# Two masked-attention layers in overlapped turns: layer 1's statistics and norms moved into the next turn, the second reciprocal behind the last addition

## The chip, the core and the metric

The kernel runs on one core of one Trainium2 chip. The metric is device time in microseconds (us). Five engines matter: PE (TensorE, the matrix products; its weight loads are listed as PEld), DVE (VectorE), ACT (ScalarE), POOL (GpSimd) and SP (SyncE), which issues every DMA of this kernel. Each engine works through its own instructions in the order in which the program lists them, and waits at an instruction until what that one needs is there. So an instruction that waits holds up everything behind it on its engine.

## What is computed

The input `x` is 128 graphs of 128 nodes with 512 features, `adj` is a 0/1 mask of 128x128 for each graph. Two layers follow one another; cut to what matters they are

```
# layer 0: 4 heads of 64; mask = adj
q, k, v = x @ Wq, x @ Wk, x @ Wv
x = layernorm(x + softmax(where(mask, q k^T / 8, -max)) v @ Wo + bo)
# layer 1: 8 heads of 64; mask = adj | identity
h = (x - mean) * rsqrt(var + eps) * gamma + beta
q, k, v = split(h @ w_qkv^T)
x = layernorm(x + softmax(where(mask, q k^T / 8, -1e9)) v @ w_out^T + b_out)
```

All arithmetic is in 32-bit floats.

## The kernel before

**Groups and turns.** Two graphs make a group, so there are 64 groups. The loop runs over turns `s`. One turn works on several groups at different stages, which are independent of one another: layer 0's q, k, v of group s (`product_0`), layer 0's scores and softmax of group s-1 (called part 0), layer 0's attention output and norm of group s-2, layer 1's q, k, v of group s-3 (`qk`, `v`), layer 1's scores and softmax of group s-4 (parts 1 and 2, one for each graph), and layer 1's output of group s-5. `opening` fills the pipeline, `step(s)` runs for s = 2 to 63, `closing(s)` for s = 64 to 66, and `last` ends it. From turn 6 on `step` has all its stages; those 58 turns are most of the time.

**The order is written out by hand.** The scheduler is off (`tc.manual_schedule()`), so the order of the calls in `step` is the order of the instructions on each engine. A buffer that is given again (a pool's tag with its number of buffers) makes its new writer wait for the old readers, DMAs included.

**Products in seven parts.** Every large product is cut into quarters and done with seven half-sized products instead of eight (numbers 1 to 7). `INTO` says in which PSUM bank each is summed: 1, 6, 7 and 4 are summed one after another in bank "a", 5 and 3 in "f", 2 in a bank of its own. After each product somebody takes the partial sum out of the bank: so 4 may start only when the sum of 7 has been read. For the output products (`out_product`, PE on line 498) the reader is DVE, which adds the bank to the rows `R[g]` (line 502). For `product_0` (PE on line 460) ACT copies 1, 6, 5 and 4 (lines 469, 471) and DVE adds 2, 7 and 3 (line 474). For layer 1's `qk` and `v` (line 338) ACT and DVE share it likewise (lines 347, 374, 362). In the profile the output product 4 is `oa<-wso,aT`, and product 4 of `product_0` is `a<-xT,ws` and `a<-ws,xT`.

**Softmax.** `masked` (DVE, line 565) copies the scores out of PSUM under the mask, `maxima` (DVE, line 571) takes row maxima, `exps` (ACT, line 580) eight exponentials for each part in two halves with their row sums, `normalised` a reciprocal of the sums (DVE, line 588) and a multiplication (POOL, line 589). `blocks` transposes blocks of 32 on DVE (line 604) and `put`s them to memory (SP, line 214, `scrp`); `probs_arrive` fetches them in transposed order in four DMAs (SP, line 220, `pT`). Layer 1's k and q go the same way (`scrk`, `kt`, `scrq`, `rawq`), and `q_in_order` (ACT, line 412) puts q in order for the next turn's scores of part 1 (`sc_a`, line 536). The rows of x and of layer 0's result are turned in the same manner by `turn` (DVE, line 229) and fetched by `arrive` (`raw`). The tiles that `turn` and `blocks` write share one tag with two buffers, taken in turn: `blocks(s, 1)` writes the buffer that `blocks(s, 0)` put to memory.

**Statistics and norms.** `stats(l, g, b)` is one `bn_stats` and one `bn_aggr` on DVE (lines 682, 683) for graph b of the group; after b = 1 `roots` computes the scale and the shift in four short POOL instructions (lines 690 to 705). `norms` is put on a list, `later`, and issued by the next `flush()`: two ACT instructions (line 716) and, for layer 1, the DMA of the finished rows to the output (SP, line 719). `step` has two flushes: in the old order the first writes layer 1's norms of the turn before, the second layer 0's of this turn. `load_rows(s - 1)` (SP, line 80) reads x again into one of five row buffers, the one whose rows that output DMA has just written out, so it waits until that DMA has landed. `with_self` (DVE, line 544) adds the diagonal to a mask. `finish` (ACT, line 268) prepares layer 1's input, `addend` (POOL, line 671) adds the bias to the rows.

Of the kernel before, what the change touches and what calls it, by code (L numbers as in the profile page):

```python
# [27 lines left out]
def kernel(ctx: ExitStack, tc: tile.TileContext, x, adj, wq, wk, wv, wo, bo,  # L28
# [4 lines left out]
    NG = B // G  # L33
# [23 lines left out]
    def flush(what=later):  # L57
        while what:
            what.pop(0)()
# [17 lines left out]
    def load_rows(g):  # L77
        if 0 <= g < NG and g not in R:
            R[g] = five.tile([P, G, E], F32, tag="r", name=f"r_{g}")
            nc.sync.dma_start(R[g], x[g * G:(g + 1) * G].rearrange("b n e -> n b e"))  # L80
# [178 lines left out]
    def finish(g, half):  # L259

        if not 0 <= g < NG:
            return
        raw = RAW[1]
        if half == 0:
            XT[1, g] = one.tile([P, KC, T], F32, tag="xT1", name=f"xT1_{g}")
        xT = XT[1, g]
        for c in range(half * KH, (half + 1) * KH):
            nc.scalar.activation(xT[:, c, :].rearrange("p (b a j) -> p b a j", b=G, a=4),
                                 raw[:, :, :, c, :].rearrange("p a b j -> p b a j"),
                                 AF.Identity, bias=gb[:, KC + c:KC + c + 1], scale=gb[:, c:c + 1])  # L270
        if half == 1:
            sums(1, g)
# [268 lines left out]
    def with_self(g):  # L541

        if 0 <= g < NG:
            nc.vector.tensor_tensor(M[g], M[g], eye[:, None, :].to_broadcast([P, G, N]), op=ALU.max)

    def cleared(s, *parts):

        for part in parts:
            if group_of(s, part) is not None:
                sm = SM[part] = one.tile([P, 2, K1, N], F32, tag=f"sm{part}", name=f"sm{part}_{s}")  # L550
                nc.gpsimd.memset(sm, NEG1 if part else NEG0)  # L551
# [22 lines left out]
    def exps(s, part, *halves):  # L574
        if group_of(s, part) is None:
            return
        sm, nmax, total = SM[part], NMAX[part], TOTAL[part]
        for i in halves:
            for k in range(K1):
                nc.scalar.activation(sm[:, i, k, :], sm[:, i, k, :], AF.Exp, bias=nmax[:, i, k:k + 1],  # L580
                                     accum_out=total[:, i, k:k + 1])

    def normalised(s, *parts):
        for part in parts:
            if group_of(s, part) is None:
                continue
            rec = one.tile([P, 2, K1], F32, tag=f"rec{part}", name=f"rec{part}_{s}")
            nc.vector.reciprocal(rec, TOTAL[part])  # L588
            nc.gpsimd.tensor_tensor(SM[part], SM[part], rec[:, :, :, None].to_broadcast([P, 2, K1, N]),  # L589
                                    op=ALU.mult)  # L590
# [7 lines left out]
    def blocks(s, *parts):  # L598


        for part in parts:
            if group_of(s, part) is not None:
                t = one.tile([P, 4, 2 * K1 * 32], F32, tag="turned", bufs=2, name=f"turnedp{part}_{s}")
                nc.vector.transpose(t.rearrange("p q (h r) -> p q h r", r=32),  # L604
                                    SM.pop(part).rearrange("p i k (q r) -> p q (i k) r", r=32))
                SCR["p", part] = put(t, f"scrp{part}_{s}")
# [50 lines left out]
    def out_sums(l, g):  # L657
        if not 0 <= g < NG:
            return
        K = HEADS[l] // 2  # L660
        so = SO[l, g] = one.tile([P, 4, K // 2, N], F32, tag=("qo0", "xs0")[l], name=f"so{l}_{g}")
        halves_sums(so, AT[l, g].rearrange("p b (h c) n -> p b h c n", h=2))
# [13 lines left out]
    def stats(l, g, b):  # L676
        if not 0 <= g < NG:
            return
        if b == 0:
            MV[l, g] = two.tile([P, G, nc.vector.BN_AGGR_DIM], F32, tag="mv", name=f"mv{l}_{g}")  # L680
        st = three.tile([P, nc.vector.BN_STATS_DIM], F32, tag="st", name="st")
        nc.vector.bn_stats(st, R[g][:, b])
        nc.vector.bn_aggr(MV[l, g][:, b], st)  # L683
        if b == G - 1:
            roots(l, g)
# [125 lines left out]
    def step(s):  # L811

        made = scores(s)
        load_ahead(s + 1)
        if s > 2:
            in_order(s)
            sums(0, s)
        arrive(1, s - 3)
        masked(made, s, 0, 1, 2)
        attend(s)  # L820
        maxima(s, 0, 1)
        out_sums(0, s - 2)
        exps(s, 0, 0)
        product_0(s, 1)
        exps(s, 0, 1)
        out_product(0, s - 2, 1, 2, 5)
        maxima(s, 2)
        product_0(s, 2)
        flush()
        load_rows(s - 1)  # L830
        normalised(s, 0)
        out_product(0, s - 2, 6, 3)
        exps(s, 1, 0)
        stats(0, s - 2, 0)
        product_0(s, 6)
        exps(s, 1, 1)
        normalised(s, 1)
        finish(s - 3, 0)
        out_product(0, s - 2, 7)
        product_0(s, 5)  # L840
        out_product(0, s - 2, 4)
        blocks(s, 0)
        stats(0, s - 2, 1)
        exps(s, 2, 0)
        product_0(s, 7)
        finish(s - 3, 1)
        exps(s, 2, 1)
        product_0(s, 3)
        turn(0, s + 1)
        normalised(s, 2)  # L850
        product_0(s, 4)
        if s in (2, 3):
            prepare(len(setup) - (s == 2))
        blocks(s, 1)
        probs_arrive(s, 0)
        qk(s - 3, 1)
        if s == 2:
            weight_sums(w1qk, wsqk, 1)
            prepare(1)
        flush()  # L860
        qk(s - 3, 2)
        blocks(s, 2)
        arrive(0, s + 1)
        probs_arrive(s, 1)
        qk(s - 3, 6, 5)
        flush(latest)
        addend(1, s - 5)
        out_sums(1, s - 5)
        qk(s - 3, 7, 3, 4)
        k_arrive(s - 3, 0)  # L870
        probs_arrive(s, 2)
        turn(1, s - 2)
        out_product(1, s - 5, 1, 2)
        q_arrive(s - 3)
        v(s - 3, 1, 2)
        k_arrive(s - 3, 1)
        cleared(s + 1, 0, 1, 2)
        out_product(1, s - 5, 6)
        v(s - 3, 6, 5)
        out_product(1, s - 5, 5)  # L880
        v(s - 3, 7, 3)
        out_product(1, s - 5, 7)
        q_in_order(s - 3)
        v(s - 3, 4)
        out_product(1, s - 5, 3, 4)
        addend(0, s - 1)
        stats(1, s - 5, 0)
        stats(1, s - 5, 1)
        with_self(s - 2)
        if s == 2:  # L890
            weight_sums(w1v, wsv, 0, 1)
        if s == 3:
            weight_sums_out(1)

    def closing(s):

        made = scores(s)
        arrive(1, s - 3)
        masked(made, s, 0, 1, 2)
        attend(s)  # L900
        maxima(s, 0, 1)
        finish(s - 3, 0)
        out_sums(0, s - 2)
        exps(s, 0, 0)
        out_product(0, s - 2, 1, 2, 5)
        maxima(s, 2)
        flush()
        load_rows(s - 1)
        finish(s - 3, 1)
        qk(s - 3, 1)  # L910
        exps(s, 0, 1)
        out_product(0, s - 2, 6, 3)
        qk(s - 3, 2)
        normalised(s, 0)
        exps(s, 1, 0)
        out_product(0, s - 2, 7, 4)
        stats(0, s - 2, 0)
        stats(0, s - 2, 1)
        qk(s - 3, 6)
        exps(s, 1, 1)  # L920
        addend(1, s - 5)
        out_sums(1, s - 5)
        qk(s - 3, 5)
        normalised(s, 1)
        exps(s, 2, 0)
        blocks(s, 0)
        flush()
        qk(s - 3, 7)
        exps(s, 2, 1)
        turn(1, s - 2)  # L930
        blocks(s, 1)
        probs_arrive(s, 0)
        qk(s - 3, 3)
        normalised(s, 2)
        flush(latest)
        cleared(s + 1, 0, 1)
        qk(s - 3, 4)
        probs_arrive(s, 1)
        out_product(1, s - 5, 1, 2)
        k_arrive(s - 3, 0)  # L940
        q_arrive(s - 3)
        k_arrive(s - 3, 1)
        blocks(s, 2)
        if s < NG + 2:
            v(s - 3, 1)
        out_product(1, s - 5, 6, 5)
        if s < NG + 2:
            v(s - 3, 2, 6, 5)
        out_product(1, s - 5, 7)
        probs_arrive(s, 2)  # L950
        out_product(1, s - 5, 3, 4)
        q_in_order(s - 3)
        if s < NG + 2:
            v(s - 3, 7, 3, 4)
        stats(1, s - 5, 0)
        stats(1, s - 5, 1)
        cleared(s + 1, 2)
        addend(0, s - 1)
        with_self(s - 2)
# [46 lines left out]
    for s in range(NG, NG + 3):  # L1006
        closing(s)
# [30 lines left out]
```

## Time and profile before

| | us |
|---|---|
| median of 3 runs | 3039.32 (3038.34 to 3039.86) |
| time of the profiled execution | 3041.11 |
| its span, first to last instruction | 3039.3 |
| PE busy | 2838.4 (93%) |
| DVE busy | 1927.0 (63%) |
| POOL busy | 1744.8 (57%) |
| ACT busy | 1543.1 (51%) |
| 16 DMA engines, mean busy share of the one queue | 62.7% |

The profile is of one execution. Its page gives sums over the span; the trace behind it can be asked for the waits of each engine, for the rows of one engine in a stretch of time, and for the busy times, the granted PE clock and the share of the DMA engines in any stretch. In rows of the timeline the columns are start, duration, engine, line, operation, what is written from what, shapes, count, and in brackets the idle time of the engine just before and what ended it. Durations of neighbouring instructions overlap a little, so where a chain is added up here, it goes by the distance from one start to the next.

### The profile page before, as it was taken

The page shows a single profiled execution, that of the slowest core. Times are in us where ns is not written, and L with a number is a line of the kernel's source. Part 1 is how long each engine was busy: PE and PEld are TensorE (multiplying, and loading weights), DVE is VectorE, ACT ScalarE, POOL GpSimd, SP SyncE. Part 2 cuts the span into 40 slices and gives each one's busy share as a digit, 9 for nine tenths or more (in the row PEclk, how much of TensorE's full clock was granted, in tenths as well). Part 3 has the DMA queues.
Part 4 walks back from the last instruction along what each step waited for, and adds up shares of the span by engine and source line. Part 5 has one row for each costly group of instructions (what it writes and reads, how often), then busy time and mean ns, then how long its engine had stood idle before and what let it go on. Part 6 is the DMA issues. An engine that isn't in the chain of part 4 may idle for free.

```text
span 3039.3 us, 54138 instructions
## 1 busy us (share of the span) xinstructions
PE 2838.4 (93%) x18077; PEld 2234.4 (74%) x18077; DVE 1927.0 (63%) x3545; ACT 1543.1 (51%) x4871; POOL 1744.8 (57%) x2311
## 2 busy tenths in 40 slices
PE   8899999999999999999999999999999999999987
PEld 7677777777777777777777777777777777777766
DVE  6566666666666666666666666666666666666644
ACT  3355455454554554554554545545545545445444
POOL 4455555655655655555556556556555555565554
PEclk9999999999999999999999999999999999999998
DMA  5666766756657657667567567676675675675541
GB/s 169 186 178 187 216 183 187 214 177 194 211 178 202 199 178 216 185 185 217 183 184 216 179 191 210 178 205 197 179 216 183 187 218 181 187 213 177 166 141 61
DMA packets 482790, 570.93 MB, mean 188 GB/s; under 512 B 60872, under 2 KB 383440, under 8 KB 482512
## 3 DMA queue, kind: packets, MB, share of 16 engines
q1 hardware_dynamic: 482512, 567.46, 62.7%
q8 instruction: 145, 2.38, 0.3%
q14 instruction: 133, 1.09, 0.1%
HBM read 304.09 MB, written 263.19 MB: 187 GB/s over the span
## 4 chain that ended last, share of the span: by engine, by line
PE 67%; ACT 17%; DVE 7%; issue 3%; SPq 2%; DMA 2%; POOL 2%; ACTq 0%; POOLq 0%; DVEq 0%
PE qka L338 14%; ACT sm L580 12%; PE oa L498 8%; PE qkf L338 7%; PE a L460 6%; PE va L338 6%; PE av L650 6%; PE qkc L338 4%; PE of L498 3%; PE vf L338 3%; ACT r L716 3%; PE f L460 2%; DVE nmax L571 2%; SPq L220 2%; PE sc L536 2%
## 5 line engine op out<-in xcount | busy, mean ns | idle before, releaser
L580 ACT ACTIVATE sm<-sm,nmax 128x128 f32<-128x128 f32 x1536 | 596.4, 393 | 56.2 <-POOL so L302 43.0
L589 POOL TENSOR_TENSOR sm<-sm,rec 128x1024 f32<-128x1024 f32 x192 | 364.0, 1896 | 342.7 <-DVE rec L588 342.7
L671 POOL TENSOR_TENSOR r<-r,bias 128x1024 f32<-128x1024 f32 x128 | 301.2, 2353 | 222.1 <-ACT r L670 222.1
L690 POOL TENSOR_SCALAR ve<-mv 128x2 f32<-128x2 f32 x191 | 41.4, 217 | 562.1 <-DVE mv L683 556.7
L347 ACT COPY ev<-va 128x256 f32<-128x256 f32 x128 | 47.6, 372 | 513.4 <-PE va L338 513.4
L502 DVE TENSOR_TENSOR r<-oa,r 128x256 f32<-128x256 f32 x508 | 206.2, 406 | 152.0 <-PE oa L498 142.0
L580 ACT ACTIVATION_READ_ACCUMULATOR sm<-sm,nmax 128x1 f32 x1536 | 294.4, 192 | 0.0
L412 ACT ACTIVATE qo<-rawq 128x512 f32<-128x512 f32 x124 | 71.3, 621 | 350.3 <-DMA rawq<-scrq 350.3
L502 DVE TENSOR_TENSOR r<-of,r 128x256 f32<-128x256 f32 x254 | 107.3, 422 | 217.7 <-PE of L498 211.1
L498 PE MATMUL oa<-wso,aT 128*128 128x256 f32 x380 | 111.5, 403 | 138.8 <-DVE r L502 138.8
L604 DVE STREAM_TRANSPOSE turnedp<-sm 128x1024 f32<-128x1024 f32 x189 | 229.1, 1212 | 18.6 <-POOL sm L589 15.3
L338 PE MATMUL qkf<-w,xs 128*128 128x512 f32 x496 | 233.2, 592 | 0.5 <-ACT eqk L347 0.5
L338 PE MATMUL qka<-wsqk,xs 128*128 128x512 f32 x496 | 233.1, 592 | 0.0
L571 DVE TENSOR_REDUCE nmax<-sm 128x8 f32<-128x1024 f32 x192 | 226.5, 1206 | 0.2
L302 POOL TENSOR_TENSOR xs<-xT 128x256 f32<-128x256 f32 x256 | 186.7, 729 | 69.1 <-ACT xT L256 37.6
L498 PE MATMUL oa<-wso,so 128*128 128x256 f32 x760 | 210.0, 386 | 12.6 <-DVE r L502 7.9
L498 PE MATMUL of<-wo,so 128*128 128x256 f32 x760 | 209.8, 386 | 0.9 <-POOL so L302 0.7
L716 ACT ACTIVATE r<-r,shift,root 128x512 f32<-128x512 f32 x254 | 192.2, 805 | 0.4 <-POOL shift L705 0.4
L498 PEld LDWEIGHTS oa<-wso,aT 128*128 128x128 f32 x380 | 67.7, 191 | 157.8 <-DVE r L502 151.0
L338 PEld LDWEIGHTS qkf<-w,xs 128*128 128x128 f32 x496 | 94.2, 190 | 119.4 <-issue 117.9
L338 PEld LDWEIGHTS qka<-wsqk,xs 128*128 128x128 f32 x496 | 94.3, 190 | 118.2 <-issue 117.7
L551 POOL MEMSET sm<- 128x1024 f32 x192 | 175.1, 951 | 0.0
(178 smaller groups left out, 7178.7 us busy)
## 6 DMA issues: line engine op xcount, KB each, us to landing
scrp<-turnedp SPq DMA_DIRECT2D x189, 512.0 KB, 3.1
pT<-scrp SPq DMA_DIRECT2D x756, 128.0 KB, 3.6
scr<-turned SPq DMA_DIRECT2D x125, 512.0 KB, 3.6
raw<-scr SPq DMA_DIRECT2D x500, 128.0 KB, 3.6
r<-in_x_dram SPq DMA_DIRECT2D x63, 512.0 KB, 3.6
out_dram<-r SPq DMA_DIRECT2D x63, 512.0 KB, 2.8
scrk<-tk SPq DMA_DIRECT2D x124, 256.0 KB, 3.0
scrq<-tq SPq DMA_DIRECT2D x62, 512.0 KB, 3.8
```

The lines of the kernel that those rows point to most:

```text
L302: nc.gpsimd.tensor_tensor(o, a0, a1, op=op)
L338: nc.tensor.matmul(o, lhsT, rhs, start=first and m == 0, stop=m == len(todo) - 1, skip_group_check=True)
L460: nc.tensor.matmul(acc[:, at * P:(at + 1) * P], lhsT, rhs, start=first and n == 0, stop=n == len(todo) - 1, skip_group_check=True)
L498: nc.tensor.matmul(acc, left[:, c], right[:, c], start=first and c == 0, stop=c == hk - 1, skip_group_check=True)
L502: nc.vector.tensor_add(part, acc, part)
L571: nc.vector.tensor_reduce(NMAX[part], SM[part], AX.X, ALU.max, negate=True)
L580: nc.scalar.activation(sm[:, i, k, :], sm[:, i, k, :], AF.Exp, bias=nmax[:, i, k:k + 1], accum_out=total[:, i, k:k + 1])
L589: nc.gpsimd.tensor_tensor(SM[part], SM[part], rec[:, :, :, None].to_broadcast([P, 2, K1, N]), op=ALU.mult)
L604: nc.vector.transpose(t.rearrange("p q (h r) -> p q h r", r=32), SM.pop(part).rearrange("p i k (q r) -> p q (i k) r", r=32))
L650: nc.tensor.matmul(pm[i * D:(i + 1) * D, at, :].rearrange("p (a r) -> p a r", r=32), v, pT[:, :, i * K1 + at, :], start=True, stop=True)
L671: nc.gpsimd.tensor_tensor(R[g], R[g], (bias0, bias1)[l][:, None, :].to_broadcast([P, G, E]), op=ALU.add)
L716: nc.scalar.activation(R[g][:, b], R[g][:, b], AF.Identity, bias=shift[:, b:b + 1], scale=root[:, b:b + 1])
```

## The change

It reorders `step` and adds two calls to `closing`; no instruction is added, removed or changed in kind.

- Layer 1's `stats` no longer stand at the end of turn s (for group s-5) but in turn s+1 (there group s-6), behind the output products 6 and 3 of layer 0. The first `flush()` with its norms and output DMA, and `load_rows`, move from before `normalised(s, 0)` to behind the output product 4 of layer 0.
- `normalised(s, 1)`, and `finish(s - 3, 0)` with it, move from before the output product 7 to the same place, behind the output product 4.
- Layer 0's first `stats` move from before `product_0(s, 6)` to beside the second, and `blocks(s, 0)` moves behind both and behind `exps(s, 2, 0)` in the text.
- `with_self` moves from the turn's end to before layer 1's output product 6.
- `closing(64)` does the statistics that turn 63 used to do.

```diff
@@ step(s)
         product_0(s, 2)
-        flush()
-        load_rows(s - 1)
         normalised(s, 0)
         out_product(0, s - 2, 6, 3)
         exps(s, 1, 0)
-        stats(0, s - 2, 0)
+        stats(1, s - 6, 0)
+        stats(1, s - 6, 1)
         product_0(s, 6)
         exps(s, 1, 1)
-        normalised(s, 1)
-        finish(s - 3, 0)
         out_product(0, s - 2, 7)
         product_0(s, 5)
         out_product(0, s - 2, 4)
-        blocks(s, 0)
+        flush()
+        load_rows(s - 1)
+        normalised(s, 1)
+        finish(s - 3, 0)
+        stats(0, s - 2, 0)
         stats(0, s - 2, 1)
         exps(s, 2, 0)
+        blocks(s, 0)
         product_0(s, 7)
...
         cleared(s + 1, 0, 1, 2)
+        with_self(s - 2)
         out_product(1, s - 5, 6)
...
         out_product(1, s - 5, 3, 4)
         addend(0, s - 1)
-        stats(1, s - 5, 0)
-        stats(1, s - 5, 1)
-        with_self(s - 2)
@@ closing(s)
         out_sums(0, s - 2)
+        if s == NG:
+            stats(1, s - 6, 0)
+            stats(1, s - 6, 1)
         exps(s, 0, 0)
```

## The prediction

> **What bounds the kernel now.** I read the list of waits of PE first, because the page has PE busy 93% of the span and a matrix engine that full can only be helped where it stands still. Over the 58 full turns (6 to 63, from 193.7 to 2875.6 us by the starts of each turn's first score product, line 531: 2681.9 us, 46.24 a turn) it names one place that counts. Columns: engine, line, who is waited for, us in total, times, longest.
>
> ```profile
> PE oa L498 <- DVE r L502: 133.1, 57, 2.8
> PE a L460 <- DVE qkv L474: 6.2, 26, 0.2
> PE sc_a L536 <- ACT qo L412: 2.2, 6, 0.7
> ```
>
> PE waits some 2.3 us in each turn before an output product, for DVE's addition. Nothing else on PE is near that. The third line matters later: q for part 1's scores comes just in time already.
>
> Next the timeline of PE and DVE around one such wait.
>
> ```profile
> 1546.36 0.61 PE L460 MATMUL f<-w,xs 128*128 128x128 f32 x4
> 1549.20 0.98 PE L498 MATMUL oa<-wso,aT 128*128 128x256 f32 x2 [2.23 <-DVE r L502]
> ```
>
> ```profile
> 1544.97 0.69 DVE L682 BATCH_NORM_STATS2 st<-r 128x6 f32<-128x512 f32 x1
> 1545.70 0.18 DVE L683 BATCH_NORM_AGGREGATE mv<-st 128x2 f32<-128x6 f32 x1
> 1548.65 0.20 DVE L588 RECIPROCAL rec<-total 128x8 f32<-128x8 f32 x1 [2.77 <-ACT sm L580]
> 1548.77 0.37 DVE L502 TENSOR_TENSOR r<-oa,r 128x256 f32<-128x256 f32 x1
> ```
>
> PE has the sum of product 7 ready at 1545.64. Its addition stands on DVE behind part 1's reciprocal, which waits 2.77 us for ACT's exponentials. So product 4 waits for ACT, through DVE's order. ACT works without a break from 1540.20 to then, with layer 1's norms (1.41 us from start to start) in between.
>
> The wait costs twice. The stretches with the granted clock (first column of the kind "1.00" after the busy times) show it:
>
> ```profile
> 1546.07:1549.48 3.41, 1.18 (x10) 0.99 (x9) 0.49 (x2) 3.41 (x15) 0.57 (x2) 1.00 0.42 156
> 1549.48:1552.89 3.41, 3.41 (x16) 3.26 (x16) 2.38 (x5) 3.41 (x15) 1.54 (x2) 0.50 0.48 184
> ```
>
> A stretch of 3.41 us with PE busy for 1.18 of it is followed by one at half clock. Of the 58 turns 31 have such a stretch and take 46.76 us; 27 have none and take 45.63. Cut in such stretches of 3.41 us from 300 to 2850 us, the trace has 0.45 as the least busy share of PE before a full-clock stretch, and 0.43 as the highest before a half-clock one. A gap under 1.9 us can't bring a stretch that low.
>
> On this the Trainium skill differs ("TensorE: Matmul & The Clock Gate", section "HAM oscillation — how this bites in real kernels"): it asks for idle gaps over about 3.4 us before the clock falls, and no gap here reaches that. By it the 31 slow stretches would have another cause and stay, and the forecast below would be worse by 31 x 1.13 = 35 us. The row above decides against it.
>
> **The change, part by part.** T is the start of output product 4 on PE. A turn at full clock is 45.63 us, with PE idle 2.51 before T (1501.04 to 1503.55 in that turn) and 0.24 before `product_0`'s product 4; so 42.87 us are PE's own.
>
> *The wait at T.* Behind product 3's addition DVE now does layer 1's statistics instead of layer 0's first and the reciprocal. Both graphs take 1.61 us (1533.26 to 1534.87, start to start). From 1544.97 that is 1546.58; the addition of 7 starts there, and PE follows such an addition by 0.43 (1548.77 to 1549.20): 1547.01, where PE ends `product_0`'s product 5 at 1546.97. At the turn's start the same statistics (and `with_self`, 0.31) no longer stand before `masked`: score sums are ready at 1533.97 and `masked` started at 1535.18, so DVE gains up to 1.1 us there. I take 0 for the wait at T; the bounds are 0 and 0.1. The exponentials of part 1 lose the norms before them, end about T+0.2, and the reciprocal now reaches DVE at T+1.04, so it no longer waits.
>
> *The next wait: `product_0`'s product 4.* What DVE does between the last addition and the one that this product waits for grows. From T: two products 0.60, their addition starts at T+0.64; reciprocal +0.40; both of layer 0's statistics +0.12; `blocks(s, 0)` +1.61; the addition of `product_0`'s 7 +1.16 (1504.63 to 1505.79); PE +0.59 (1506.58 to 1507.17). Sum T+4.52. PE is there at T+3.28 (3.62 before, less the 0.24 wait and 0.10 by which the first products after an idle stretch were slower, 0.70 against 0.60). New gap 1.24 us, bounds 0.9 and 1.5 by start-to-start steps of 0.35 to 0.46 for an addition. It is under 1.9, so the clock stays.
>
> *ACT and POOL.* Layer 1's shift comes out of POOL 1.92 us after the second aggregate's start, near T+1.4; norms until T+2.85, `finish` 0.98, exponentials 1.55, `finish` 0.99, exponentials 1.55, two copies (0.45, 0.58): T+8.95. `qk` product 6 needs the last copy at T+9.39. Slack 0.4, so hidden; without it every further us would cost PE one. POOL's four sums for `qk` (0.8 apart) start at T+6.4 and the one that product 6 needs is done by T+8. Hidden. `with_self` falls into DVE's 0.37 us of idle before output product 6's addition.
>
> *The DMA queue.* This is what the change may pay with. SP's rows around T:
>
> ```profile
> 1545.23 0.39 SPq L719 DMA_DIRECT2D out_dram<-r  x1
> 1548.91 0.39 SPq L80 DMA_DIRECT2D r<-in_x_dram  x1
> 1551.82 0.34 SPq L214 DMA_DIRECT2D scrp<-turnedp  x1
> 1556.04 0.34 SPq L214 DMA_DIRECT2D scr<-turned  x1
> 1557.24 0.32 SPq L214 DMA_DIRECT2D scrp<-turnedp  x1
> ```
>
> The row load waits for the output DMA to land (median 2.84 us from issue to issue), at a time when SP has nothing else to do. Now the output DMA goes at T+2.9, the load at T+5.75, and part 0's `scrp`, whose tile is ready at T+3.95, stands behind it: T+6.2 instead of T+2.34. It lands 2.6 us later when alone (`scrp` at 1505.89) and 4.2 when packed (`x` at 1531.57): T+8.8 to T+10.4, I take 9.6. Only then may `blocks(s, 1)` write the same buffer on DVE (1.2 us; before, T+5.25): part 1's `scrp` at T+10.9 instead of T+6.46. From there SP has 7.7 us of issues before `scrq` and `scrk` and 0.4 between them: the second `scrk` at T+19.3. Its data are there at T+18.92 (T+18.03 before, plus 0.9 as PE's part from T to there grows). From this `scrk` to q's landing SP and the DMA engines have no hole (the engines are 0.98 busy from 1519 to 1533), and q had 0.1 us to spare (ready 1533.87, PE there at 1533.97). So late here is late on PE: 0.3 us by the middle, 0 by the quick landing, 1.1 by the slow one. Two more DMAs of 512 KB, out and in, now share the engines with this traffic; I add 0.2. I take 0.5.
>
> *Sum.* 42.87 + 0 + 1.24 + 0.5 = 44.61 us a turn; 58 turns 2587.4 against 2681.9: 94.5 less. Turns 4 and 5 have the moved reciprocal too; PE's waits of this kind before turn 6 come to 4.2 us in all, which I leave out. `closing(64)` gains 1.6 us of DVE work that turn 63 loses: between 0 and 1.6, taken as 0. Span 3039.3 - 94.5 = 2944.8, the profiled execution's own time 3041.1 - 94.5 = 2946.6; the runs' median of 3039.32 lies 1.8 below that execution, so **2945 us** for the median.
>
> **The rivals.**
>
> *The queue takes it without delay.* For: SP idles 1.0 us before `scrq` and 0.6 before part 2's `scrp`, and puts alone land in 2.6. Then a turn is 44.11 and the time 2916. Against: the load sits directly before the `scrp`.
>
> *Slower: the row load blocks SP's queue.* One mechanism: the load's wait for the output DMA, now behind T, pushes the `scrp` puts, then the fetches, and with them q past the start of the scores. Price 58 us for each us that q is late. The gain is eaten when q is 46.24 - 44.11 = 2.13 us late. With the slow landing (T+10.4) and 1.5 us more from bursts that share the DMA engines, q is 2.6 late: 46.71 a turn, 3067. For it: engines without a hole from 1519 to 1533. Against: before T they are nearly idle (busy share 0.15 from 1538 to 1544), and SP's own slack takes the first part.
>
> *The new gap hides too.* If PE's order or ACT's copies keep PE back elsewhere, or DVE's chain is 1.2 shorter, only 42.87 + 0.5 remain: 2872 at best. Against: each row of that chain was measured.
>
> *It doesn't do what it says.* The wait at T could belong to something else than the reciprocal. The row with 2.77 us of idle and the release by ACT directly before it excludes that nearly; if ACT's exponentials then held `product_0` through its copies, the turn would stay near 46.2 and the time near 3037.
>
> **How the numbers follow.** Forecast, 2930 to 2985: 0.50. Queue without delay, 2905 to 2930: 0.23. New gap hidden, below 2905: 0.05. q later by 1.2 to 2.0, 2985 to 3033: 0.07. No change: 0.05. Slower by the queue: 0.10. The range from 2900 to 3010 leaves out the hidden gap, half of the late q and the last two, 0.2 in all. A measurement of this kernel can tell about 0.2%, 6 us, from no change. Faster 0.85, same 0.05, slower 0.10.
>
> **What would show it.** In the new trace: DVE's reciprocal of part 1 without idle time before it; no wait of PE at `oa<-wso,aT` and one of 0.9 to 1.5 us at `a<-xT,ws` for DVE's `qkv`; no stretch at half clock in the full turns, so a mean clock near 1.00; `scrp` behind the row load, some 3.9 us later after T than now, and DVE's second `turnedp` waiting for its landing; PE's wait at `sc_a` for ACT's `qo` up from 2.2 us to about 29 in total. I am wrong if that last one is over 120 us, or if ACT's copies release PE in `qk`.

## The result and the profile after

The changed kernel takes 3261.62 us (median of 4 runs, 3257.28 to 3268.38) against 3038.83 us: a ratio of 1.0741, 95% interval 1.0715 to 1.0768. It is slower by 223 us, where the forecast was 2945 us, faster by 94, with a range up to 3010.

The waits of PE in the full turns of the profile after (192.0 to 3094.4 us, 50.04 a turn; columns as before):

```profile
PE sc_a L536 <- ACT qo L412: 219.7, 57, 5.1
PE a L460 <- DVE qkv L474: 64.6, 58, 1.5
```

The wait before the output product 4, 133.1 us before, is gone from the list, as meant. The wait for DVE at `product_0`'s product 4 is 1.11 us a turn. But PE now waits 3.8 us in each turn at `sc_a` for q, where it waited 2.2 us in all. The stretches around one such wait say what else it costs (after the busy times: granted clock, DMA share, GB/s):

```profile
1496.50:1499.90 3.40, 0.00 (x0) 0.00 (x0) 1.33 (x2) 0.00 (x0) 0.00 (x0) 1.00 0.95 222
1499.90:1503.30 3.40, 2.58 (x23) 2.58 (x25) 0.41 (x1) 2.44 (x5) 0.69 (x1) 0.53 0.70 229
1503.30:1506.70 3.40, 3.40 (x34) 3.17 (x34) 3.04 (x5) 0.12 (x1) 2.17 (x4) 0.50 0.29 83
```

PE stands still through a whole stretch, with the DMA engines 0.95 busy, and then runs at half clock for two. The full turns hold 57 such slow spells, 20 of one stretch and 37 of two, 5.5 us a turn at half clock; before it were 31, all of one stretch, and 1.8 us.

Where q's lateness comes from is read from SP's and DVE's rows of one turn (T, the start of output product 4 on PE, is 1516.49):

```profile
1519.25 0.40 SPq L719 DMA_DIRECT2D out_dram<-r  x1
1522.07 0.39 SPq L80 DMA_DIRECT2D r<-in_x_dram  x1
1522.55 0.42 SPq L214 DMA_DIRECT2D scrp<-turnedp  x1
1523.06 0.38 SPq L214 DMA_DIRECT2D scr<-turned  x1
1528.86 0.32 SPq L214 DMA_DIRECT2D scrp<-turnedp  x1
```

```profile
1517.47 0.19 DVE L588 RECIPROCAL rec<-total 128x8 f32<-128x8 f32 x1
1519.15 1.23 DVE L604 STREAM_TRANSPOSE turnedp<-sm 128x1024 f32<-128x1024 f32 x1
1524.27 0.20 DVE L588 RECIPROCAL rec<-total 128x8 f32<-128x8 f32 x1 [1.78 <-ACT sm L580]
1527.59 1.25 DVE L604 STREAM_TRANSPOSE turnedp<-sm 128x1024 f32<-128x1024 f32 x1 [3.12 <-DMA scrp<-turnedp]
```

Part 0's blocks are ready at 1520.4. Their put waits until 1522.55, behind the row load, which waits for the output DMA. It lands 4.92 us later, and DVE stands idle 3.12 us for that landing, since part 1's blocks go into the same buffer. The second `scrp` is then 12.4 us behind T.

The turn adds up: 42.87 us of PE's own, 1.11 and 3.83 of waits make 47.81, which leaves 2.2 us to 50.04. The half clock accounts for them: PE is busy for 4.64 us a turn of the time at half clock, work that full clock would do in half of that, 2.3 us less.

### The profile page after: what moved, and what is told of

It reads as the page before. It is cut to its first block, busy times and chain, and to the rows that moved or that the text cites. A ratio compares the mean times of both kernels' runs of the same rounds, so it can differ in the third digit from the quotient of the medians.

```text
span 3260.2 us, 54135 instructions
## 1 busy us (share of the span) xinstructions
PE 2918.0 (90%) x18077; PEld 2306.4 (71%) x18077; DVE 1931.4 (59%) x3545; ACT 1536.9 (47%) x4871; POOL 1744.8 (54%) x2311
## 4 chain that ended last, share of the span: by engine, by line
PE 59%; DMA 17%; SPq 8%; DVE 7%; issue 5%; POOL 2%; ACT 2%; DVEq 0%; ACTq 0%; POOLq 0%
PE qka L338 10%; PE a L460 8%; DMA rawq<-scrq 7%; SPq L220 7%; PE av L650 6%; PE oa L498 6%; PE qkf L338 5%; PE sc L536 3%; PE va L338 3%; DMA scrp<-turnedp 3%; PE sc_a L536 3%; PE qkc L338 3%; PE of L498 3%; PE c L460 2%; PE f L460 2%
## 5 line engine op out<-in xcount | busy, mean ns | idle before, releaser
L536 PE MATMUL sc_a<-kt,qo 64*128 64x128 f32 x512 | 125.2, 418 | 227.5 <-ACT qo L412 226.5
L536 PEld LDWEIGHTS sc_a<-kt,qo 64*128 64x128 f32 x512 | 107.1, 307 | 240.0 <-ACT qo L412 238.6
L565 DVE COPY_PREDICATED sm<-m,sc 128x512 f32<-128x512 uint8 x256 | 171.5, 723 | 64.6 <-PE sc L531 45.3
L565 DVE COPY_PREDICATED sm<-m,sc_a 128x512 f32<-128x512 uint8 x64 | 46.8, 732 | 267.4 <-PE sc_f L536 254.2
L302 POOL TENSOR_TENSOR so<-aT 128x256 f32<-128x256 f32 (+1 forms) x254 | 150.2, 591 | 75.5 <-ACT aT L653 75.5
```

The source lines that it names most:

```text
L302: nc.gpsimd.tensor_tensor(o, a0, a1, op=op)
L536: nc.tensor.matmul(ps[h % 2][:, h // 2, :].rearrange("p (a j) -> p a j", j=32), QO[g, b][r, h // 2], keys_of(g, b, h // 2, r), start=True, ...
```

## The experiments

Three theories stood against each other. **Q**: the row load's wait in SP's queue, now behind T, delays the puts, and the two-buffer tile passes the delay on to q. **D**: the output DMA and the row load share the DMA engines with the fetches for q, in whatever order they are issued. **B**: DVE and ACT do their work for the probabilities later (moved reciprocal, statistics, blocks), so the puts are late anyway.

The table has medians of 50 turns (9 to 58), in us from T, and PE's mean wait at `sc_a` in a turn; how late q is means that wait. The turn that the prediction started from is one of the 27 at full clock, where the second `scrp` goes at T+6.46; the medians of the row "before" mix them with the slow ones. Ratios are to runs of the kernel before on the same chip, whose medians are 3033.1, 3035.6 and 3037.2 us.

| kernel | output DMA | row load | first scrp | part 1's blocks | second scrp | second scrk | first rawq | wait at sc_a | time |
|---|---|---|---|---|---|---|---|---|---|
| before | -3.97 | -1.13 | 2.34 | 6.81 | 8.03 | 19.14 | 24.29 | 0.04 | 3038.8 |
| changed | 2.77 | 5.60 | 6.08 | 11.13 | 12.41 | 21.73 | 28.33 | 3.83 | 3261.6 |
| three_turned | 2.76 | 5.58 | 6.06 | 7.90 | 9.13 | 19.83 | 26.08 | 1.98 | 3076.6 |
| load_later | 2.77 | 6.45 | 3.91 | 7.90 | 9.17 | 18.79 | 25.04 | 0.85 | 2960.7 |
| six_rows | 2.78 | before T | 3.91 | 7.91 | 9.18 | 18.79 | 24.88 | 0.73 | 2956.4 |
| flush_alone | 2.25 | 5.08 | 5.57 | 10.64 | 11.92 | 21.28 | 27.86 | 4.20 | 3306.2 |
| recip_alone | -1.69 | 1.16 | 3.09 | 7.28 | 8.51 | 18.77 | 24.38 | 0.17 | 2916.4 |
| extra_bytes | -2.41 | 0.60 | 2.55 | 8.06 | 9.34 | 18.90 | 24.81 | 1.51 | 2994.4 |

### load_later: the row load behind the puts

```diff
         flush()
-        load_rows(s - 1)
         normalised(s, 1)
...
         turn(0, s + 1)
+        load_rows(s - 1)
```

> The changed kernel with one line moved: the row load stands behind the put of part 0's blocks and the put of the turned x, instead of before both. Theory Q (the load's wait for the output DMA blocks SP's queue): from T, the output DMA goes at T+2.8, part 0's scrp at about T+3.9 instead of T+6.1, the load at T+6.6 without waiting, part 1's blocks at T+7.9 instead of T+11.1. PE's wait at sc_a for q falls from 3.83 us a turn to 0 to 0.5; a turn takes 44.0 to 44.6 us and the time is 2905 to 2950 us. Rival D (the output DMA and the row load share the DMA engines with the fetches, in whatever order): the same bytes move in the same stretch, q stays late by 2 us or more, time over 3040. Rival B (DVE and ACT do their work for the probabilities later, so the puts are late anyway): part 1's scrp at T+9.1 is still 2.6 later than before, q late by 1 to 2 us, time 2980 to 3100.

Measured: 2960.68 us, ratio to the kernel before 0.9762 (0.9744 to 0.9779). SP's and DVE's rows of one turn (T = 1417.32), and PE's waits from 193 to 2800 us:

```profile
1420.09 0.39 SPq L719 DMA_DIRECT2D out_dram<-r  x1
1421.23 0.34 SPq L214 DMA_DIRECT2D scrp<-turnedp  x1
1423.34 0.33 SPq L214 DMA_DIRECT2D scr<-turned  x1
1423.77 0.39 SPq L80 DMA_DIRECT2D r<-in_x_dram  x1
```

```profile
1425.11 0.20 DVE L588 RECIPROCAL rec<-total 128x8 f32<-128x8 f32 x1 [1.79 <-ACT sm L580]
1425.23 1.23 DVE L604 STREAM_TRANSPOSE turnedp<-sm 128x1024 f32<-128x1024 f32 x1
```

```profile
PE a L460 <- DVE qkv L474: 64.4, 58, 1.5
PE sc_a L536 <- ACT qo L412: 48.2, 55, 2.0
```

The load finds the output DMA landed and waits for nothing; the blocks follow their reciprocal without idle time. One line in SP's order carries some 300 us, and Q holds for these. The move takes away two things at once: part 0's put goes 2.17 us sooner, and it lands in 2.96 us instead of 4.87 (medians), with no row load just ahead of it. How the 300 us divide between the two isn't shown. q is still 0.85 late, more than Q's 0.5, and the time lies 11 us above Q's range; D and B as main causes would have left it at 2980 or more.

### three_turned: a third buffer for the turned tiles

```diff
-t = one.tile([P, 4, ...], F32, tag="turned", bufs=2, ...)
+t = one.tile([P, 4, ...], F32, tag="turned", bufs=3, ...)
...
-    bias1 = const.tile([P, E], F32, name="bias1")
-    nc.sync.dma_start(bias1, b_out[None, :].to_broadcast([P, E]))
+    bias1 = bias0
```

> The changed kernel with three buffers instead of two for the tiles that blocks and turn write; SP's order is that of the changed kernel. To make room it leaves out layer 1's own bias and adds layer 0's in its place. Theory Q has two steps, the late put and the buffer that waits for it: without the second, part 1's blocks start at T+7.9 instead of T+11.1 and its scrp goes at T+9.1 instead of T+12.4; q is late by 0 to 1 us, time 2905 to 2980. If instead the late put of part 0 alone delays what follows in SP's queue (no buffer in it), the time stays at 3240 to 3270. Rival D: bytes unchanged, over 3040.

Measured: 3076.59 us (two runs, 3068.63 and 3084.54), ratio 1.0142 (1.0104 to 1.018). Part 1's blocks start at T+7.9 as expected, but q is 1.98 late, not 0 to 1: the fetch of part 0's probabilities waits in SP's queue for the same landing, until T+11.04, where load_later issues it at T+9.59. So the late put acts in two ways. Taken in this order, the third buffer gives 185 of the 305 us between the changed kernel and six_rows, and the load's place in the queue the other 120. The time fits D's "over 3040" too; it is load_later and six_rows that speak against D.

### six_rows: a row load that has nothing to wait for

```diff
-R[g] = five.tile([P, G, E], F32, tag="r", name=f"r_{g}")
+R[g] = five.tile([P, G, E], F32, tag="r", bufs=6, name=f"r_{g}")
...
         product_0(s, 2)
+        load_rows(s - 1)
         normalised(s, 0)
...
         flush()
-        load_rows(s - 1)
```

(with `bias1 = bias0` as above)

> The changed kernel with six row buffers instead of five and the row load at its old place in the text, where it now finds a buffer whose rows were written out a turn earlier, so it waits for no DMA. To make room it leaves out layer 1's own bias and adds layer 0's in its place. Theory Q: nothing stands before part 0's scrp but the output DMA, scrp at about T+3.9, q late by 0 to 0.5 us, time 2905 to 2950. Rival D keeps part of the loss, as the output DMA still runs at T+2.8: 2980 to 3100. Rival B: 2980 to 3100.

Measured: 2956.36 us, ratio 0.9745 (0.9723 to 0.9768). That is 6 us above Q's range, and within 0.15% of load_later, which keeps the load behind T: in these two it makes no difference where the load stands, as no put waits behind it. Like load_later it keeps a wait at `sc_a`, 0.73 us.

### recip_alone: the reciprocal's move by itself

```diff
         exps(s, 1, 1)
-        normalised(s, 1)
-        finish(s - 3, 0)
         out_product(0, s - 2, 7)
         product_0(s, 5)
         out_product(0, s - 2, 4)
+        normalised(s, 1)
+        finish(s - 3, 0)
         blocks(s, 0)
```

> The kernel before with one part of the change alone: part 1's reciprocal, with its multiplication and the first half of finish, behind output product 4. Statistics, flush and row load stay where they were. All theories: the wait at T is gone. The exponentials of part 1 still have layer 1's norms before them, so the reciprocal waits until about T+1.9, and product 4 of product_0 waits about 1.3 us for the chain behind it. Theory Q: output DMA and row load run before T, part 0's scrp at about T+3.4, q is not late; a turn takes 44.2 us, time 2915 to 2940. Rival B, by which the later reciprocal itself delays the puts: q late by 1 us or more, time over 2975.

Measured: 2916.36 us, ratio 0.9612 (0.9595 to 0.963), in the range forecast. PE's waits from 193 to 2753 us:

```profile
PE a L460 <- DVE qkv L474: 35.3, 58, 1.0
PE sc_a L536 <- ACT qo L412: 9.1, 22, 1.0
```

The wait at `product_0`'s product 4 is 0.61 us a turn, half of the 1.3 expected. Most of the gain that the change could bring is in these two lines. A late reciprocal isn't the cause: it comes even later here (T+1.73, changed kernel 0.98) and q is nearly on time. The statistics and blocks of B stay in place here; load_later has them moved, and is 44 us slower. There the second `scrk` goes when it goes here (18.79 and 18.77), and q falls behind only after it. Which of B's moves or the output DMA's traffic makes these 44 us isn't shown.

### flush_alone: flush and row load moved by themselves

```diff
         product_0(s, 2)
-        flush()
-        load_rows(s - 1)
         normalised(s, 0)
...
         out_product(0, s - 2, 4)
+        flush()
+        load_rows(s - 1)
         blocks(s, 0)
```

> The kernel before with one other part of the change alone: the first flush and the row load stand behind output product 4; statistics, reciprocal and blocks stay. Theory Q: the norms no longer stand before the exponentials, so the wait at T shrinks by 1.4 us to about 1; but the output DMA goes at T+2.1, the load at T+5.0, part 0's scrp at T+5.4, it lands near T+10.3, part 1's scrp at T+11.6, and q is 3.0 to 4.5 us late as in the changed kernel; with a half-clock stretch in each turn about 50 us a turn, time 3200 to 3290. Rival B (the moved statistics and blocks do the harm): no loss here, 2960 to 3040.

Measured: 3306.24 us, ratio 1.0898 (1.0876 to 1.0919), a little above Q's range. PE's waits in its full turns:

```profile
PE sc_a L536 <- ACT qo L412: 238.6, 58, 5.1
PE oa L498 <- DVE r L502: 50.3, 58, 0.9
```

The first line is the whole wait of the changed kernel and some more, without its statistics, reciprocal or blocks; the second is what the norms' going leaves of the old wait. So B is out as the cause of the loss.

### extra_bytes: the traffic without the wait

```diff
         finish(s - 3, 0)
+        extra = dram.tile([P, G, E], F32, tag="extra", name=f"extra_{s}")
+        nc.sync.dma_start(extra, x[:G].rearrange("b n e -> n b e"))
         blocks(s, 0)
```

> recip_alone with one more DMA in each turn that nobody waits for: 512 KB of x copied to unused memory, issued behind output product 4, where the changed kernel issues its output DMA. It adds work that the reference has not. Rival D alone is measured so: as many bytes as the output DMA, written and read, in the same stretch, and no wait in SP's queue. Theory Q: SP pays 0.4 us for the issue, q comes at most 0.5 us later, time 2916 to 2950. Rival D: the fetches behind it slow down, q 1 us or more later, 2975 to 3050.

Measured: 2994.37 us, about 78 us over recip_alone; ratio to the kernel before 0.9858 (0.984 to 0.9876): inside the ranges of rival D. q is 1.51 us late instead of 0.17. DVE's waits, over the span:

```profile
DVE turnedp L604 <- DMA scrp<-turnedp: 72.6, 48, 3.9
```

So D is real as well: with bytes that nobody waits for just ahead of it, part 0's put lands 5.53 us after its issue instead of 3.42 (medians), and the same buffer passes it on (DVE's wait in recip_alone: 1.3 us in the full turns). The 78 us say what this copy costs at this place, not what share the output DMA has in the loss of the changed kernel.

### stats_later, blocks_first, fetch_later: is q tied to T?

stats_later is load_later with

```diff
-        stats(0, s - 2, 0)
-        stats(0, s - 2, 1)
         exps(s, 2, 0)
...
         product_0(s, 3)
+        stats(0, s - 2, 0)
+        stats(0, s - 2, 1)
         turn(0, s + 1)
```

> load_later with layer 0's two statistics moved behind the last addition of product_0, so that DVE's chain from the output product 4 to product_0's product 4 is 1.6 us shorter and PE's gap of 1.11 us there goes. If PE's gaps add up independently: q stays 0.85 late, 43.8 us a turn, 2895 us. If q is tied to T by ACT and the DMA queue (the exponentials of part 2, then blocks, scrp, the fetches), PE only arrives 1.1 us earlier at the same q and waits for it there: sc_a waits 1.7 to 2.1 us a turn, time 2945 to 2970.

Measured: 3012.57 us, ratio 0.993 (0.991 to 0.995): 52 us slower than load_later, and outside both expectations. PE's gap at `product_0`'s product 4 went. In its place stand 1.4 us a turn at `qk`'s product 6, and 1.08 at `sc_a` in the full turns. Over the span:

```profile
PE sc_a L536 <- ACT qo L412: 65.8, 60, 3.3
PE qka L338 <- POOL ve L690: 41.9, 58, 0.7
PE qka L338 <- ACT eqk L347: 39.6, 58, 0.7
```

The line with ACT's `eqk` is the copy whose slack the prediction put at 0.4 us. Shortening DVE there used that slack up. Waits of 2.49 us in the full turns against 1.93 in load_later explain 0.6 of the 0.9 us by which the turn grew (45.75 against 44.89); the rest isn't assigned.

blocks_first is recip_alone with

```diff
         out_product(0, s - 2, 4)
+        blocks(s, 0)
         normalised(s, 1)
         finish(s - 3, 0)
-        blocks(s, 0)
-        stats(0, s - 2, 1)
...
         product_0(s, 3)
+        stats(0, s - 2, 1)
```

> recip_alone with blocks of part 0 before the reciprocal (so it is done while DVE would wait for ACT) and layer 0's second statistics behind product_0's product 3. PE's gap at product_0's product 4 (0.61 us a turn in recip_alone) goes. If gaps add up independently: 43.5 us a turn, 2880 us. If q is tied to T: sc_a waits 0.6 to 0.9 us instead of 0.17, 43.9 us a turn, 2900 to 2915 us.

Measured: 2932.79 us, ratio 0.9664 (0.965 to 0.9679), 16 us slower than recip_alone and above both expectations. The gap of 0.61 us went, q is 1.04 us late (0.6 to 0.9 expected), and 0.34 came at `qk`: PE comes to q sooner and waits there. So q doesn't follow PE. That it is tied to what stands before it in SP's queue is what the next run tests.

fetch_later is blocks_first with

```diff
         k_arrive(s - 3, 0)
-        probs_arrive(s, 2)
         turn(1, s - 2)
...
         k_arrive(s - 3, 1)
+        probs_arrive(s, 2)
```

> blocks_first with the fetch of part 2's probabilities (four DMAs, 1.8 us of SP) behind the fetches of q and k instead of before them. If q is late because of what stands before it in SP's queue, q comes 1.8 us earlier and the wait at sc_a goes; the probabilities now land near T+32, where PE wants them at T+32 too, so 0 to 0.8 us may come back there: 2860 to 2895 us. If q is late because the DMA engines are full, moving one fetch behind it gains less: 2895 to 2915 us.

Measured: 2901.39 us, ratio 0.9562 (0.9546 to 0.9578). No wait at `sc_a` is left in the full turns, so four fetches out of q's way were enough, as by the first expectation, and no wait for the probabilities came in its place. The time, though, lies in the range of the second, since PE now waits elsewhere, 0.57 us at `qk` (0.34 in blocks_first) and 0.31 at `product_0`. The expectation of the next run puts both down to copies behind ACT's exponentials:

```profile
PE qka L338 <- POOL ve L690: 33.1, 58, 0.6
PE f L460 <- ACT e L469: 17.8, 58, 0.3
```

### norms_early: the flush the other way

fetch_later with

```diff
         out_sums(0, s - 2)
+        flush()
+        load_rows(s - 1)
         exps(s, 0, 0)
...
         product_0(s, 2)
-        flush()
-        load_rows(s - 1)
         normalised(s, 0)
```

> fetch_later with the first flush and the row load moved the other way, to before part 0's exponentials, where ACT idles about 1.0 us for the row maxima. The norms (1.41 us) then stand 1.0 us less in the way of the exponentials, output DMA and row load run where the DMA engines are nearly idle. Theory Q with ACT as the next bound (in fetch_later PE waits 0.31 us a turn for a copy behind part 1's exponentials and 0.57 us for one behind part 2's): both waits go, 43.1 to 43.4 us a turn, 2845 to 2870 us. If ACT is not what holds PE there: 2895 to 2905 us. If the place of the row load in SP's queue did not matter, no difference either.

Measured: 2837.3 us (5 runs, 2836.7 to 2840.55), ratio 0.9343 (0.9331 to 0.9356): the best version here, 6.6% faster than the kernel before and 13% faster than the changed one. ACT's rows show the norms in what was idle time (1.02 us before the first exponential in a turn of fetch_later):

```profile
1264.14 0.58 ACT L655 COPY aT<-av 128x512 f32<-128x512 f32 x1 [0.23 <-PE av L650]
1264.62 1.52 ACT L716 ACTIVATE r<-r,shift,root 128x512 f32<-128x512 f32 x2
1266.05 0.39 ACT L580 ACTIVATE sm<-sm,nmax 128x128 f32<-128x128 f32 x1
```

The row load, at 1269.04, waits for the output DMA (1266.21) as ever, but the next put is only due at 1274.35. In the full turns PE waits for one thing, 0.25 us a turn. The waits that went make 0.62 us; the turn became 1.12 us shorter (42.89 against 44.00), so 0.5 us of it isn't assigned, and the time came out below the 2845 expected.

## Why the prediction was wrong

The step that failed is the term for the DMA queue: 0.5 us a turn for q's lateness, measured 3.83. The clock's loss that follows from it, 2.2 us, stood at nothing. The prediction's own sign of being wrong, over 120 us in total at `sc_a`, came with 219.7.

- **What bounds the kernel, and the wait at T**: right. The wait is gone (the longest left in the full turns is 0.05 us), and recip_alone turns it into 117 us (from 3033.1 to 2916.4).
- **The next wait**: 1.24 us forecast, 1.11 measured, at the place named.
- **ACT and POOL**: hidden in the changed kernel, as forecast; the slack was as small as said (stats_later).
- **The DMA queue**: the mechanism was right, step by step, and so were its first times: output DMA T+2.9 (measured 2.77), load 5.75 (5.60), `scrp` 6.2 (6.08). The size failed: q 0.5 us late was taken, 3.83 came. Three terms were too small. *The landing*: 9.6 was taken, between 2.6 and 4.2 us after the issue; part 1's blocks started at 11.13, past the bound of 10.4: the put is issued 0.48 us behind a load of the same size and lands 4.87 us later, where load_later's has no row load just ahead of it and takes 2.96. That is 1.5 us. *SP's issues from the second `scrp` to the second `scrk`*: 8.4 us taken from the rows before, 9.3 measured, as fetches issue more slowly there (four `raw` fetches 3.08 us against 2.35). 0.9 us. *From `scrk` to the fetch of q*: held to be as in the turn that it started from, 5.73 us (the median of the kernel before is 5.15), where 6.60 was measured. 0.87 us, where 0.2 had been added. With the 0.3 that the middle case already had, these make 3.6, 0.2 less than measured. SP's rows, first of the kernel before, then of the changed one:

```profile
1521.58 0.52 SPq L384 DMA_DIRECT2D scrk<-tk  x1
1527.31 2.31 SPq L220 DMA_DIRECT2D rawq<-scrq  x4
1562.07 2.35 SPq L220 DMA_DIRECT2D raw<-scr  x4
```

```profile
1532.81 3.08 SPq L220 DMA_DIRECT2D raw<-scr  x4
1538.54 0.52 SPq L384 DMA_DIRECT2D scrk<-tk  x1
1545.07 2.24 SPq L220 DMA_DIRECT2D rawq<-scrq  x4
```

- **The clock**: the forecast had the half-clock stretches gone. That the 31 of before came from the wait at T was right: recip_alone and load_later, without that wait, have none in their full turns. The rule for falling holds too: cut in the same way, the trace after has 0.45 as the highest busy share before a half-clock stretch and 0.51 as the lowest before a full-clock one. But a wait of 3.8 us brought the half clock back in nearly every turn, 2.2 us, and for longer, as a half-clock stretch in which PE is busy for too little is followed by another.
- **The slower rival** was this mechanism with q 2.6 us late, 3067 us and a chance of 0.10. Its point of decision, 2.13 us, was too high: three_turned, with 1.98, is already 1.4% slower, as long waits bring half-clock stretches too (25 of its 58 turns have one). So its price of 58 us for each us was too low (from load_later to the changed kernel 2.98 us of wait cost 301, some 100 for each), and its chance too small. The bound of the landing came from rows in which the transfer was alone or next to small ones; and durations measured with holes in the queue were used for a queue without holes.

Taken one by one against 3033 to 3039 us: the reciprocal -117 us, the flush and the row load +271, all of the change +223. The two parts add up to +154; what the moved statistics and blocks do by themselves was not run, so the difference isn't assigned.

## What to carry to other kernels

A DMA that waits in an in-order queue costs what is queued behind it, so before moving one, write down the next entries and who waits for each; at a place where the next entry is due only later, the same wait holds up nothing (norms_early). Where one of two buffers passes a late put on to the next writer, the delay reaches further. And when data come with no slack, as q does here, price their lateness with the busy queue's durations, not with those of the idle one.

## What the hardware showed unexpectedly

A put of 512 KB that landed 2.63 us after issue when alone (1505.89 in the kernel before) landed after 4.92 when issued 0.48 us behind a load of the same size (1522.55 in the changed one). The half clock came in 57 of 58 turns with a pause of PE of 3.8 us on average, in 25 with 2.0 (three_turned), and in none with 0.85 and 1.1 us at two places of a turn (load_later). Full clock came back only after a busier stretch than the one that had lost it: of the half-clock stretches of the changed kernel, cut as in the prediction from 300 to 3045 us, all 35 with PE busy for 0.84 or less were followed by another at half clock, and all 54 with 0.86 or more by one at full clock. The other traces with such spells agree but for one stretch of extra_bytes, which was 0.91 busy and still followed by half clock.
